# Small per-row numbers of a graph dilation moved from VectorE to GpSimd, one comparison moved between two multiplications, and a joined layer-norm statistic

## The chip, the cores and the metric

The kernel runs on 1 core of one Trainium2 chip. The metric is the device time in microseconds (us) of one execution; of the kernel before there are three timed runs, and one further execution that the hardware profiler recorded. Engines are called by the profile's names: PE (TensorE matmul), PEld (TensorE weight load), DVE (VectorE), ACT (ScalarE), POOL (GpSimd) and SP (SyncE, which issues DMAs).

## The reference

The input is x of shape 16 x 1024 x 128, a dense adjacency of 16 x 1024 x 1024 in f32 with many zeros, and a node mask. Two layers follow each other, each with a layer norm in front and a residual.

```python
h = relu(layernorm(x))
q, k, v = heads(h @ Wq.T + bq), heads(h @ Wk.T + bk), heads(h @ Wv.T + bv)   # 8 heads of 16
attn = softmax(where(adj == 0, -inf, q @ k.T / 4)) * adj
attn = attn / (attn.sum(-1) + 1e-8)
x = x + merge(attn @ v) @ Wo.T + bo

h = relu(layernorm(x))
keep = dilate(adj > 0)            # row after row, see below
for i in 1, 2, 3:                 # SAGE layers on adj * keep
    out = (adj_d @ h / max(adj_d.sum(-1), 1)) @ Wr[i] + h @ Wx[i] + b[i]
    h = batchnorm(relu(out / norm(out))) ; collect h
x = x + concat(h1, h2, h3) @ Wl + bl
```

The dilation goes through the 1024 rows of a batch in turn. Row n has num neighbours; with num > 10 every sf-th of them (sf = (num+1)//2, counted along the row) is removed, with 1 < num <= 10 all are; a removed pair is removed in the row and in the column, so that earlier rows change later ones.

## The kernel before

**Attention.** The outer loop runs over 16 batches b, two halves c of the query columns and eight blocks m of 128 key rows; in each of these 256 turns two groups g of four heads follow each other. That makes 512 steps. In a step PE puts the mask and the scores of four heads into PSUM (L554, L560), ACT takes two exponentials e of 128 x 1024 (L598), DVE multiplies both by the transposed adjacency, giving two weighted exponentials w (L603), and PE multiplies these with the values one step later (L487, and L492 for the small epsilon term). A score tile of the next step is already made while this goes on. Beside it, in pieces, lie the transposes of the adjacency (L505), the next batch's layer norm and projections (`prepare`) and the last half's output projection (`conclude`).

**Dilation.** It runs beside attention as a generator that hands out pieces of DVE work (`dilation`, from L651). All 16 batches are worked on together, in 8 blocks k of 128 rows. A block has three parts:

- Its beginning: products and scans along the diagonal block (L749 to L797), and small numbers per row and batch, 128 x 16 each (`total`, `most`, `half`, `onw`, L774 to L786).
- Seven rounds (L806). A round takes the counts `gone` that PE made (L842), forms num and y from them (L819, L820), from these the position `at16` (L823 to L827), and compares the 128 x 2048 tile w with it (L836, `hit`). PE sums `hit` into the next counts. Some rounds are full ones: they also form `vb` (L830 to L834), by which PE weights two further sums (L846, L847). Full are rounds 2 and 6 in blocks 0 to 4, rounds 0, 2, 4, 6 in block 5, and all in blocks 6 and 7.
- After an end step (L854 to L865) and some wide products, the scan part: for each of the 16 batches a scan over the row (L900), ACT's positions (L915), DVE's removals (L924 to L937) and PE's transposes (L907).

**What sets the order.** PE, ACT and DVE have an order written out by hand; POOL and SP are ordered by the framework. `beside_attention` (L951) runs attention step by step. After each it takes pieces of the dilation as long as their summed cost is behind the share of attention that is done. A piece ends with a `yield` of its cost, of a mark (1: wait for the next attention step; "A" or "B": wait for a step of that parity), and for a comparison also "counts", which makes the next scores stand on PE ahead of the counts. So in the kernel before a round's small numbers and its comparison stand on DVE in front of the step's two w.

**Layer norm.** `layer_norm_relu` takes bn_stats and bn_aggr on DVE for each of eight tiles of 128 x 128, two per step (L274, L276), adds epsilon (L281), takes the power -0.5 on POOL (L282), and ends with the shift on DVE (L284) and the ReLU on ACT (L288).

**The rest.** After attention the three SAGE layers and the output follow (L1107 to L1406); the change does not touch them.

Of the kernel before, what the change touches and what calls it, by code (L numbers as in the profile page):

```python
# [16 lines left out]
ALU = mybir.AluOpType  # L17
# [4 lines left out]
P = 128  # L22
LN_EPS = 1e-5
# [3 lines left out]
ROUNDS = 7  # L27
# [7 lines left out]
def swept(ctx: ExitStack, tc: tile.TileContext, t: dict, out: bass.AP, flag: bass.AP):  # L35
# [8 lines left out]
    nc = tc.nc  # L44
# [122 lines left out]
    def first_part(p1):  # L167
# [100 lines left out]
        def layer_norm_relu(dst, src, name, lo=0, hi=NB):  # L268

            st = shared.tile([P, NB, 6], F32, name=f"st_{name}_{lo}", tag="lnst", bufs=2)  # L270
            mv = shared.tile([P, NB, 2], F32, name=f"mv_{name}_{lo}", tag="lnmv", bufs=2)
            for i in range(lo, hi, 2):
                for j in range(i, i + 2):
                    nc.vector.bn_stats(st[:, j, :], src[:, j, :])  # L274
                for j in range(i, i + 2):
                    nc.vector.bn_aggr(mv[:, j, :], st[:, j, :])  # L276
                if i + 2 < hi:
                    yield False
            rs = shared.tile([P, 2, NB], F32, name=f"rs_{name}_{lo}", tag="lnrs", bufs=2)
            n = slice(lo, hi)  # L280
            nc.vector.tensor_scalar(rs[:, 1, n], mv[:, n, 1], LN_EPS, None, ALU.add)  # L281
            nc.gpsimd.tensor_tensor(rs[:, 0, n], rs[:, 1, n], minus_half[:, n], ALU.pow)  # L282
            yield False
            nc.vector.scalar_tensor_tensor(rs[:, 1, n], mv[:, n, 0], -1.0, rs[:, 0, n], ALU.mult, ALU.mult)  # L284
# [178 lines left out]


        beside = []

        def take_on(steps, at):
            beside.insert(at, [steps, next(steps)])
# [11 lines left out]
        def attention():  # L480
# [86 lines left out]
            for i, (b, c, m) in enumerate(turns):  # L567
# [12 lines left out]
                for g in range(2):  # L580
                    scs = scores(i, g)
                    go_on_with(f"half {c}")
                    if g == 0:
                        go_on_with("first")
                        turning = turn_over(i + 2)
                        next(turning, None)
                    else:
                        go_on_with(True)
                    if late:
                        values(*late)  # L590
                    elif g == 0:
                        go_on_with(True)
                    if (i, g) == (2, 0):
                        node_masks()
                    es, ws = [], []
                    for q in range(2):
                        e = pool.tile([P, 2, HN], F32, name=f"e_{b}_{c}_{m}_{g}_{q}", tag="e", bufs=4)
                        nc.scalar.activation(e, scs[q], AF.Exp, scale=1.0 / math.sqrt(HD))  # L598
                        es.append(e)
                    go_on_with("evict by VectorE")  # L600
                    for q in range(2):
                        w = pool.tile([P, 2, HN], F32, name=f"w_{b}_{c}_{m}_{g}_{q}", tag="w", bufs=4)
                        nc.vector.tensor_tensor(w, es[q], aT.to_broadcast([P, 2, HN]), ALU.mult)  # L603
                        ws.append(w)
                    late = (acc, v1, m, g, es, ws)
                    if m == 0 and g == 0 and i > 0:

                        take_on(conclude(*done), 1 if c == 0 else 0)
                        go_on_with(False)
                    go_on_with("evict")  # L610
                    if g == 0:
                        next(turning, None)
                    go_on_with(False)
                    if i + g + 1 < len(turns):
                        made["next"] = partial(scores, i + g, 1 - g)
                    yield
# [23 lines left out]
        def twice(ap):  # L640

            return ap.unsqueeze(2).to_broadcast([P, B, 2])

        def over_rows(pairs):

            return pairs.unsqueeze(2).to_broadcast([P, B, P // 2, 2])

        def in_pairs(tile_):
            return tile_.rearrange("p b (i t) -> p b i t", t=2)

        def dilation():  # L651
# [84 lines left out]
            for k in range(NB):  # L736
# [32 lines left out]
                for c, hb in enumerate(halves):  # L769
# [1 line left out]
                    for b in range(B // 2):  # L771
                        nc.tensor.transpose(pd[:, b, :], dgs[c][:, b, :], ident_bf)
                    if c == 0:
                        nc.vector.tensor_scalar(onw, w[:, :, P - 1], 1024.0, None, ALU.subtract)  # L774
                        for dg, of in zip(dgs, halves):
                            nc.vector.tensor_reduce(last1[:, of], dg, AX.X, ALU.add)
                    else:

                        nc.vector.tensor_tensor(total, left, right, ALU.add)
                        nc.vector.tensor_tensor(total, total, last1, ALU.add)  # L780
                        nc.vector.tensor_tensor(most, total, kill[:, :, k], ALU.add)
                        nc.vector.tensor_tensor(onw, onw, right, ALU.add)
                        nc.vector.scalar_tensor_tensor(half, total, -0.5, onw, ALU.mult, ALU.add)
                        nc.vector.tensor_scalar(half, half, 0.25, None, ALU.add)
                        end16 = small.tile([P, B, 2], F16, name=f"end16_{k}", tag="at16", bufs=2)
                        nc.vector.tensor_scalar(end16, twice(onw), 1024.0, None, ALU.add)  # L786
# [16 lines left out]
                nc.vector.tensor_copy(mosts, most)  # L803
                nc.vector.tensor_copy(mids, half)
                full = {2, ROUNDS - 1} if k < 5 else {0, 2, 4, ROUNDS - 1} if k == 5 else set(range(ROUNDS))
                for r in range(ROUNDS):  # L806

# [1 line left out]
                    v = small.tile([P, 5, B], F32, name=f"v_{k}_{r}", tag="v", bufs=2)  # L809
                    num, y, c, high, lost = (v[:, i, :] for i in range(5))  # L810
                    if gone is None:
                        nc.vector.tensor_copy(num, most)
                        nc.vector.tensor_copy(y, half)
                    else:
                        if r - 1 in full:
                            rest = gone[:, B : 2 * B]
# [2 lines left out]
                        nc.vector.tensor_tensor(num, mosts, gone[:, :B], ALU.subtract)  # L819
                        nc.vector.scalar_tensor_tensor(y, gone[:, :B], 0.5, mids, ALU.mult, ALU.add)  # L820
                    if r == ROUNDS - 1:
                        nc.vector.tensor_copy(prev, num)
                    nc.vector.tensor_scalar(c, y, MAGIC, MAGIC - 5120.0, ALU.add, ALU.subtract)  # L823
                    nc.vector.tensor_scalar(high, num, 10.5, None, ALU.is_gt)

                    at16 = small.tile([P, B, 2], F16, name=f"at16_{k}_{r}", tag="at16", bufs=2)
                    nc.vector.scalar_tensor_tensor(at16, twice(high), -4096.0, twice(c), ALU.mult, ALU.add)  # L827
                    if r in full:
                        vb = small.tile([P, 2, B, 2], BF, name=f"vb_{k}_{r}", tag="vb", bufs=2)
                        nc.vector.scalar_tensor_tensor(  # L830
                            vb[:, 0], twice(num), 1.5, twice(high), ALU.is_gt, ALU.subtract
                        )
                        nc.vector.scalar_tensor_tensor(c, y, 5120.0, c, ALU.add, ALU.is_gt)
                        nc.vector.tensor_tensor(vb[:, 1], twice(c), twice(high), ALU.mult)  # L834
                    yield (1.6 if r in full else 1.0), (1 if r in (1, 3) else 0)
                    nc.vector.tensor_tensor(in_pairs(hit), in_pairs(w), over_rows(at16), ALU.is_equal)  # L836
                    yield 1.3, 1, "counts"


                    gone = ps_d.tile([P, 512], F32, name=f"gone_{k}_{r}", tag="d")  # L840
# [19 lines left out]
                nc.vector.tensor_scalar(num, num, 0.5, 0.25, ALU.mult, ALU.add)  # L860
                nc.vector.tensor_scalar(num, num, MAGIC, MAGIC, ALU.add, ALU.subtract)
                nc.vector.tensor_scalar(at_odd, num, -3.0, None, ALU.mult)
                nc.vector.tensor_scalar(at_even, num, -3.0, 2.0, ALU.mult, ALU.add)
                nc.vector.scalar_tensor_tensor(off, num, 1.0, high, ALU.add, ALU.mult)
                nc.vector.tensor_scalar(off, off, -1.0, None, ALU.add)  # L865
# [1112 lines left out]
```

## Time and profile before

| What | Value |
|---|---|
| three timed runs, median (lowest, highest) | 3397.52 us (3397.18, 3398.41) |
| the profiled execution's own time | 3396.91 us |
| its span, first to last instruction | 3395.1 us |
| granted TensorE clock | 0.995 |
| two w of a step, each (L603), 1024 of them | 1219 ns, 1205.5 us in all |
| exponential (L598), 1024 of them | 1022 ns, 991.9 us in all |
| comparison of a round (L836), 56 of them | 1219 ns, 68.2 us in all |
| at16 of a round on DVE (L827), 56 of them | 193 ns |
| bn_aggr (L276), 256 of them | 173 ns |
| power on POOL (L282), 33 of them | 65.5 us in all |
| cast of 128 x 16 on POOL (L410), 64 of them | 198 ns |

The page of the profile gives for each engine its busy time as a share of the span, then the span in 40 slices, the DMA queues, the chain that ended last, and the costliest groups of instructions. In this case the chain covers only the last DVE instructions, so that it says nothing of attention. The windows view gives each engine's busy time in a stretch, the timeline gives single instructions in order of time (start, length, engine, line, what it writes and reads, and in brackets the idle time before it with what ended it). Attention's first w starts at 21.1 us, the last at 2321.3 us.

### The profile page before, as it was taken

How to read it: one execution, taken by the hardware profiler on the slowest of the kernel's cores; microseconds unless marked ns; L12 is line 12 of the kernel's file. 1: busy time of each engine (PE TensorE's matmuls, PEld its weight loads, DVE VectorE, ACT ScalarE, POOL GpSimd, SP SyncE). 2: the span in 40 equal slices, each digit the busy share in tenths (PEclk: the TensorE clock that was granted, in tenths of full speed). 3: DMA queues.
4: the chain of work that ended last, by engine and by line, in shares of the span. 5: the costliest groups of instructions: out<-in, count | busy, mean ns of one | idle time of the engine just before them, and what ended most of it. 6: DMA issues, size and time to landing. Idle time of an engine off the chain costs nothing. (4 is left out here: it accounts for less than half of the span.)

```text
span 3395.1 us, 86338 instructions
## 1 busy us (share of the span) xinstructions
PE 3310.6 (98%) x34855; PEld 1872.4 (55%) x34855; DVE 3025.5 (89%) x5399; ACT 2305.4 (68%) x3909; POOL 164.2 (5%) x253
## 2 busy tenths in 40 slices
PE   8999999999999999999999999999999899999997
PEld 3333333333333333333334334336999899999997
DVE  7898989989989998998998999897888899988887
ACT  7699689779879969968976986884232344423334
POOL 2000000000000000000000000000000000000000
PEclk9999999999999999999999999999999999999999
DMA  7357456547637736845863773677999799989996
GB/s 242 108 168 206 137 149 199 161 129 221 188 122 213 221 122 183 238 144 158 236 190 122 237 240 119 189 228 261 346 341 343 284 353 350 353 323 350 352 351 222
DMA packets 650123, 772.28 MB, mean 227 GB/s; under 512 B 173264, under 2 KB 569168, under 8 KB 637424
## 3 DMA queue, kind: packets, MB, share of 16 engines
q1 hardware_dynamic: 632672, 708.58, 64.4%
q0 software_dynamic: 15456, 57.30, 5.0%
q8 instruction: 275, 4.51, 0.6%
q14 instruction: 136, 1.11, 0.1%
q10 hardware_dynamic: 1584, 0.79, 0.1%
HBM read 508.50 MB, written 157.29 MB: 196 GB/s over the span
## 5 line engine op out<-in xcount | busy, mean ns | idle before, releaser
L603 DVE TENSOR_TENSOR w<-e,aT 128x1024 f32<-128x1024 f32 x1024 | 1205.5, 1219 | 138.4 <-ACT e L598 136.8
L598 ACT ACTIVATE e<-sc 128x1024 f32<-128x1024 f32 x1024 | 991.9, 1022 | 333.6 <-PE sc L560 332.6
L1132 PE MATMUL pg<-y,aT 128*128 128x128 f32 (+1 forms) x6144 | 729.8, 275 | 0.0
L1132 PEld LDWEIGHTS pg<-y,aT 128*128 128x128 f32 x6144 | 707.9, 192 | 0.0
L487 PE MATMUL acc<-w,both 128*32 128x512 f32 x4096 | 586.7, 605 | 3.1 <-DVE w L603 2.6
L560 PE MATMUL sc<-qT,kT 32*128 32x512 f32 x4096 | 584.4, 640 | 0.3 <-ACT qT L315 0.3
L492 PE MATMUL acc<-e,eps 128*32 128x512 f32 x4096 | 573.1, 592 | 0.0
L146 DVE SCALAR_TENSOR_TENSOR aT<-mr,aT 128x1024 f32<-128x1024 bf16 x384 | 458.8, 1217 | 0.0
L492 PEld LDWEIGHTS acc<-e,eps 128*32 128x32 f32 x4096 | 150.6, 110 | 294.6 <-issue 289.6
L1155 ACT ACTIVATE sq<-o 128x512 f32<-128x512 f32 x96 | 60.6, 631 | 328.5 <-DVE o L1150 328.5
L554 PEld LDWEIGHTS <-never 32*32 32x32 bf16 x8192 | 80.9, 88 | 347.9 <-issue 325.6
L554 PE MATMUL sc<-nomask,never 32*32 32x512 bf16 x8192 | 252.3, 385 | 16.8 <-ACT e L598 12.3
L1173 ACT COPY hT<-pt 128x512 f32<-128x512 f32 x96 | 56.3, 586 | 289.3 <-PE pt L1169 280.0
L560 PEld LDWEIGHTS sc<-qT,kT 32*128 32x128 f32 x4096 | 160.1, 183 | 116.9 <-issue 116.1
L505 PEld LDWEIGHTS pa<-ident,a 128*128 128x128 f32 x1024 | 107.7, 141 | 181.4 <-issue 129.7
L487 PEld LDWEIGHTS acc<-w,both 128*32 128x32 f32 x4096 | 92.8, 108 | 156.2 <-issue 65.4
L915 ACT ACTIVATE wr<-both,th 128x512 f16<-128x512 f16 x256 | 172.1, 730 | 7.1 <-DVE both L900 6.9
L505 PE MATMUL pa<-ident,a 128*128 128x128 f32 x1024 | 168.3, 287 | 6.4 <-DMA a<-in_adj 5.7
L512 ACT ACTIVATE nomask<-aT 128x512 bf16<-128x512 f32 x256 | 161.4, 630 | 8.1
L1150 DVE SCALAR_TENSOR_TENSOR o<-pg,rdeg,mine 128x128 f32<-128x128 f32 x384 | 108.1, 344 | 55.9 <-PE pg L1132 52.6
L508 ACT COPY aT<-pa 128x512 f32<-128x512 f32 x256 | 152.7, 597 | 5.3 <-PE pa L505 4.3
L900 DVE TENSOR_TENSOR_SCAN both<-rk 128x513 f16<-128x513 bf16 x128 | 155.9, 1218 | 0.0
(228 smaller groups left out, 3894.9 us busy)
## 6 DMA issues: line engine op xcount, KB each, us to landing
aT<-aT_d SPq DMA_DIRECT2D x94, 2048.0 KB, 9.9
mr<-mr_d SPq DMA_DIRECT2D x188, 512.0 KB, 6.0
aT_d<-aT SPq DMA_DIRECT2D x256, 256.0 KB, 4.0
a<-in_adj SPq DMA_DIRECT2D x253, 256.0 KB, 3.7
ad<-in_adj SPq DMA_DIRECT2D x112, 512.0 KB, 4.2
nomask<-nomask SPq DMA_DIRECT2D x512, 96.0 KB, 2.7
nomask<-nomask SPq DMA_DIRECT2D x512, 64.0 KB, 2.7
nomask<-nomask SPq DMA_DIRECT2D x512, 32.0 KB, 2.7
```

What stands on the lines that cost most here:

```text
L146: nc.vector.scalar_tensor_tensor(part, mrs[h][:, j : j + 2, :].rearrange("p j n -> p (j n)"), 0.0, part, ALU.is_equal, ALU.mult)
L487: nc.tensor.matmul(acc[g][32 * j : 32 * j + 32, :], v1[:, m, (2 * j + g) * HW : (2 * j + g) * HW + 32], ws[j // 2][:, j % 2, :], start=(m ...
L492: nc.tensor.matmul(acc[g][32 * j : 32 * j + 32, :], eps8, es[j // 2][:, j % 2, :], start=False, stop=(m == NB - 1),)
L505: nc.tensor.transpose(pa[:, k * P : (k + 1) * P], a[:, k, :], ident)
L512: nc.scalar.activation(nomask[:, 0, :], aT[:, 0, :], AF.Relu, bias=1.0, scale=-1e38, accum_out=zeros[:, i : i + 1])
L554: nc.tensor.matmul(scs[j // 2][to : to + 32, j % 2, :], never[rows, rows], nomask[rows, j, :], start=True, stop=False, tile_position=(32 * ...
L560: nc.tensor.matmul(scs[j // 2][:, j % 2, :], kT[rows, mm], qTs[c][rows, g, :], start=False, stop=True, tile_position=(32 * j, 0),)
L598: nc.scalar.activation(e, scs[q], AF.Exp, scale=1.0 / math.sqrt(HD))
L603: nc.vector.tensor_tensor(w, es[q], aT.to_broadcast([P, 2, HN]), ALU.mult)
L900: nc.vector.tensor_tensor_scan(pair_sums[b % 2], row[:, 0::2], row[:, 1::2], 0.0, ALU.add, ALU.add)
L915: nc.scalar.activation(wrs[b][:, t * HN : (t + 1) * HN], pair_sums[b % 2][:, t : t + HN], AF.Abs, bias=at[:, b : b + 1], scale=2.0,)
L1132: nc.tensor.matmul(pg[:, i // 2, at : at + width], aT[:, j, i * P : (i + 1) * P], y[:, j, :width], start=(j == 0), stop=(j == NB - 1),)
```

## The change

It has four parts.

1. The small 128 x 16 numbers of the dilation are computed by POOL: of a block's beginning, of the rounds (`c`, `high`, `at16`, `vb`) and of the end step. Where DVE had one instruction with two operations on two tensors, POOL has two. What reads PSUM (num, y, the counts) stays on DVE.
2. The comparison of a round is no longer put on DVE at once. It goes into a list `amid`, and attention takes it from there after the first w of its next step, ahead of the second w. Each round now ends with one `yield`, with mark 1, of cost 2.0 (full) or 1.7.
3. The planner's cost of a round is 1.9 instead of 2.5.
4. Layer norm has no bn_aggr: after the last bn_stats of a layer norm, six DVE instructions on 128 x 8 join the statistics of the even and the odd elements for all tiles at once.

```diff
@@ layer_norm_relu
-                for j in range(i, i + 2):
-                    nc.vector.bn_aggr(mv[:, j, :], st[:, j, :])
...
-            nc.vector.tensor_scalar(rs[:, 1, n], mv[:, n, 1], LN_EPS, None, ALU.add)
+            apart, squares = mv[:, n, 0], mv[:, n, 1]
+            nc.vector.tensor_tensor(apart, st[:, n, 1], st[:, n, 4], ALU.subtract)
+            nc.vector.tensor_tensor(squares, st[:, n, 2], st[:, n, 5], ALU.add)
+            nc.vector.scalar_tensor_tensor(apart, apart, D / 4.0, apart, ALU.mult, ALU.mult)
+            nc.vector.tensor_tensor(squares, squares, apart, ALU.add)
+            nc.vector.tensor_scalar(rs[:, 1, n], squares, 1.0 / D, LN_EPS, ALU.mult, ALU.add)
+            nc.vector.tensor_tensor(apart, st[:, n, 1], st[:, n, 4], ALU.add)
             nc.gpsimd.tensor_tensor(rs[:, 0, n], rs[:, 1, n], minus_half[:, n], ALU.pow)
@@ attention, after each w
                         ws.append(w)
+                        while q == 0 and amid:
+                            amid.pop()()
@@ dilation, a block's beginning: seven of its instructions, and L774
-                        nc.vector.tensor_tensor(total, left, right, ALU.add)
+                        nc.gpsimd.tensor_tensor(total, left, right, ALU.add)
...
@@ dilation, a round
-                    nc.vector.tensor_scalar(c, y, MAGIC, MAGIC - 5120.0, ALU.add, ALU.subtract)
-                    nc.vector.tensor_scalar(high, num, 10.5, None, ALU.is_gt)
+                    nc.gpsimd.tensor_scalar(c, y, MAGIC, MAGIC - 5120.0, ALU.add, ALU.subtract)
+                    nc.gpsimd.tensor_scalar(high, num, 10.5, -4096.0, ALU.is_gt, ALU.mult)
                     at16 = small.tile([P, B, 2], F16, name=f"at16_{k}_{r}", tag="at16", bufs=2)
-                    nc.vector.scalar_tensor_tensor(at16, twice(high), -4096.0, twice(c), ALU.mult, ALU.add)
+                    nc.gpsimd.tensor_tensor(at16, twice(high), twice(c), ALU.add)
                     if r in full:
                         vb = small.tile([P, 2, B, 2], BF, name=f"vb_{k}_{r}", tag="vb", bufs=2)
-                        nc.vector.scalar_tensor_tensor(
-                            vb[:, 0], twice(num), 1.5, twice(high), ALU.is_gt, ALU.subtract
-                        )
-                        nc.vector.scalar_tensor_tensor(c, y, 5120.0, c, ALU.add, ALU.is_gt)
-                        nc.vector.tensor_tensor(vb[:, 1], twice(c), twice(high), ALU.mult)
-                    yield (1.6 if r in full else 1.0), (1 if r in (1, 3) else 0)
-                    nc.vector.tensor_tensor(in_pairs(hit), in_pairs(w), over_rows(at16), ALU.is_equal)
-                    yield 1.3, 1, "counts"
+                        nc.gpsimd.tensor_scalar(high, num, 10.5, None, ALU.is_gt)
+                        nc.gpsimd.tensor_scalar(lost, num, 1.5, None, ALU.is_gt)
+                        nc.gpsimd.tensor_tensor(vb[:, 0], twice(lost), twice(high), ALU.subtract)
+                        nc.gpsimd.tensor_tensor(c, y, c, ALU.subtract)
+                        nc.gpsimd.tensor_scalar(c, c, -5120.0, None, ALU.is_gt)
+                        nc.gpsimd.tensor_tensor(vb[:, 1], twice(c), twice(high), ALU.mult)
+                    amid.append(
+                        partial(nc.vector.tensor_tensor, in_pairs(hit), in_pairs(w), over_rows(at16), ALU.is_equal)
+                    )
+                    yield (2.0 if r in full else 1.7), 1, "counts"
+                    while amid:
+                        amid.pop()()
@@ dilation, the end step: L857 to L865, eight instructions become ten
-                nc.vector.tensor_scalar(high, num, 10.5, None, ALU.is_gt)
-                nc.vector.scalar_tensor_tensor(allof, num, 1.5, high, ALU.is_gt, ALU.subtract)
+                nc.gpsimd.tensor_scalar(high, num, 10.5, None, ALU.is_gt)
+                nc.gpsimd.tensor_scalar(allof, num, 1.5, None, ALU.is_gt)
+                nc.gpsimd.tensor_tensor(allof, allof, high, ALU.subtract)
...
@@ beside_attention
-            block = 1.3 + 4.6 + 3.9 + 1.4 + 1.2 + 2.6 + ROUNDS * 2.5 + 2.0 + 5.1 + 1.4 + B * 4.2 + 2.4
+            block = 1.3 + 4.6 + 3.9 + 1.4 + 1.2 + 2.6 + ROUNDS * 1.9 + 2.0 + 5.1 + 1.4 + B * 4.2 + 2.4
```

More of the change, by code (lines that the diff above doesn't have):

```diff
@@ L280, in layer_norm_relu @@
             n = slice(lo, hi)
-            nc.vector.tensor_scalar(rs[:, 1, n], mv[:, n, 1], LN_EPS, None, ALU.add)
+            apart, squares = mv[:, n, 0], mv[:, n, 1]
[5 more added lines that the diff above has]
+            nc.vector.tensor_tensor(apart, st[:, n, 1], st[:, n, 4], ALU.add)
             nc.gpsimd.tensor_tensor(rs[:, 0, n], rs[:, 1, n], minus_half[:, n], ALU.pow)
             yield False
-            nc.vector.scalar_tensor_tensor(rs[:, 1, n], mv[:, n, 0], -1.0, rs[:, 0, n], ALU.mult, ALU.mult)
+            nc.vector.scalar_tensor_tensor(rs[:, 1, n], apart, -0.5, rs[:, 0, n], ALU.mult, ALU.mult)
             for i in range(lo, hi, 2):
@@ L465, in first_part @@
         beside = []
+        amid = []
         def take_on(steps, at):
@@ L773, in dilation @@
                     if c == 0:
-                        nc.vector.tensor_scalar(onw, w[:, :, P - 1], 1024.0, None, ALU.subtract)
+                        nc.gpsimd.tensor_scalar(onw, w[:, :, P - 1], 1024.0, None, ALU.subtract)
                         for dg, of in zip(dgs, halves):
@@ L777, in dilation @@
                     else:
[L779 to L784, printed above, removed]
+                        nc.gpsimd.tensor_tensor(total, left, right, ALU.add)
+                        nc.gpsimd.tensor_tensor(total, total, last1, ALU.add)
+                        nc.gpsimd.tensor_tensor(most, total, kill[:, :, k], ALU.add)
+                        nc.gpsimd.tensor_tensor(onw, onw, right, ALU.add)
+                        nc.gpsimd.tensor_scalar(half, total, -0.5, 0.25, ALU.mult, ALU.add)
+                        nc.gpsimd.tensor_tensor(half, half, onw, ALU.add)
                         end16 = small.tile([P, B, 2], F16, name=f"end16_{k}", tag="at16", bufs=2)
-                        nc.vector.tensor_scalar(end16, twice(onw), 1024.0, None, ALU.add)
+                        nc.gpsimd.tensor_scalar(end16, twice(onw), 1024.0, None, ALU.add)
                     yield (2.5 if c == 0 else 1.4), 1
@@ L802, in dilation @@
                 mosts, mids = parts[:, 0, :], parts[:, 1, :]
-                nc.vector.tensor_copy(mosts, most)
-                nc.vector.tensor_copy(mids, half)
+                nc.gpsimd.tensor_copy(mosts, most)
+                nc.gpsimd.tensor_copy(mids, half)
                 full = {2, ROUNDS - 1} if k < 5 else {0, 2, 4, ROUNDS - 1} if k == 5 else set(range(ROUNDS))
@@ L811, in dilation @@
                     if gone is None:
-                        nc.vector.tensor_copy(num, most)
-                        nc.vector.tensor_copy(y, half)
+                        nc.gpsimd.tensor_copy(num, most)
+                        nc.gpsimd.tensor_copy(y, half)
                     else:
@@ L821, in dilation @@
                     if r == ROUNDS - 1:
-                        nc.vector.tensor_copy(prev, num)
-                    nc.vector.tensor_scalar(c, y, MAGIC, MAGIC - 5120.0, ALU.add, ALU.subtract)
-                    nc.vector.tensor_scalar(high, num, 10.5, None, ALU.is_gt)
+                        nc.gpsimd.tensor_copy(prev, num)
+                    nc.gpsimd.tensor_scalar(c, y, MAGIC, MAGIC - 5120.0, ALU.add, ALU.subtract)
+                    nc.gpsimd.tensor_scalar(high, num, 10.5, -4096.0, ALU.is_gt, ALU.mult)
@@ L856, in dilation @@
                 nc.vector.tensor_tensor(changed[:, k * B : (k + 1) * B], num, prev, ALU.not_equal)
-                nc.vector.tensor_scalar(high, num, 10.5, None, ALU.is_gt)
-                nc.vector.scalar_tensor_tensor(allof, num, 1.5, high, ALU.is_gt, ALU.subtract)
[L860 to L865, printed above, removed]
+                nc.gpsimd.tensor_scalar(high, num, 10.5, None, ALU.is_gt)
+                nc.gpsimd.tensor_scalar(allof, num, 1.5, None, ALU.is_gt)
+                nc.gpsimd.tensor_tensor(allof, allof, high, ALU.subtract)
+                nc.gpsimd.tensor_scalar(num, num, 0.5, 0.25, ALU.mult, ALU.add)
+                nc.gpsimd.tensor_scalar(num, num, MAGIC, MAGIC, ALU.add, ALU.subtract)
+                nc.gpsimd.tensor_scalar(at_odd, num, -3.0, None, ALU.mult)
+                nc.gpsimd.tensor_scalar(at_even, num, -3.0, 2.0, ALU.mult, ALU.add)
+                nc.gpsimd.tensor_scalar(off, num, 1.0, None, ALU.add)
+                nc.gpsimd.tensor_tensor(off, off, high, ALU.mult)
+                nc.gpsimd.tensor_scalar(off, off, -1.0, None, ALU.add)
                 yield 2.0, 1
```

## The prediction, made blind

> **What bounds the kernel now.** I read the page first, then stage windows, then one round of the dilation in the timelines of PE and DVE, then GpSimd (POOL) beside DVE wherever POOL reads SBUF. Page, part 1, and three windows (columns: window, length, busy us of PE, PEld, DVE, ACT, POOL, clock, DMA share, GB/s):
> ```profile
> PE 3310.6 (98%) x34855; PEld 1872.4 (55%) x34855; DVE 3025.5 (89%) x5399; ACT 2305.4 (68%) x3909; POOL 164.2 (5%) x253
> 933.00:971.00 38.00, 37.86 (x532) 14.94 (x525) 35.93 (x82) 26.51 (x43) 3.39 (x4) 1.00 0.38 115
> 2061.00:2103.00 42.00, 42.00 (x713) 19.84 (x706) 38.02 (x96) 25.90 (x42) 1.42 (x4) 1.00 0.38 117
> 1889.00:2027.00 138.00, 132.49 (x1400) 49.42 (x1400) 135.75 (x215) 126.49 (x196) 7.17 (x10) 1.00 0.82 248
> ```
> The first two windows are rounds (blocks 3 and 7), the third is the scan part of block 6. In the rounds PE idles 0.14 and 0.00 us though DVE is at 95% and 91%: DVE work taken out there buys nothing by itself. Only in the scan part does PE idle (5.5 us of 138), with DVE at 98% and ACT at 92%. Attention is 512 steps from 21 to 2322 us, 4.49 us each; what lies behind it (1070 us) the change does not touch.
>
> One round, in block 3 (start us, length, engine, line):
> ```profile
> 957.49 0.55 PE L842 MATMUL gone<-one_bf,hit 128*128 128x1 bf16 x16
> 958.16 0.17 DVE L820 SCALAR_TENSOR_TENSOR v<-gone,parts 128x16 f32<-128x16 f32 x1
> 958.88 1.22 DVE L836 TENSOR_TENSOR hit<-w,at 128x2048 bf16<-128x2048 f16 x1
> 960.02 2.35 DVE L603 TENSOR_TENSOR w<-e,aT 128x1024 f32<-128x1024 f32 x2
> 960.32 0.43 PE L554 MATMUL sc<-nomask,never 32*32 32x512 bf16 x16
> 961.76 0.55 PE L842 MATMUL gone<-one_bf,hit 128*128 128x1 bf16 x16
> ```
> PE's period is 961.76-957.49 = 4.27 us. PE order is count (gone), transposes, weighted values (uses w), next scores, next count. The comparison ends at 960.10, 1.66 us before the count wants it; the two w end at 962.37, 0.37 us before the next values (962.74). That is all the slack.
>
> What POOL does when it reads SBUF beside a two-input DVE instruction:
> ```profile
> 228.47 1.22 DVE L900 TENSOR_TENSOR_SCAN both<-rk 128x513 f16<-128x513 bf16 x1
> 228.71 2.41 POOL L282 TENSOR_TENSOR rs_b<-rs_b,minus_half 128x8 f32<-128x8 f32 x1 [35.86 <-DVE rs_b L281]
> ```
> ```profile
> 896.70 2.28 DVE L756 TENSOR_TENSOR_SCAN w<-go_on,up 128x1024 f16<-128x1024 bf16 x1
> 896.96 3.45 POOL L282 TENSOR_TENSOR rs_a<-rs_a,minus_half 128x8 f32<-128x8 f32 x1 [75.42 <-DVE rs_a L281]
> ```
> ```profile
> 1472.88 1.64 POOL L282 TENSOR_TENSOR rs_a<-rs_a,minus_half 128x8 f32<-128x8 f32 x1 [75.59 <-DVE cs L779]
> ```
> The same pow takes 1.64 us beside 16-element DVE instructions, 2.41 beside a 1.22 us scan, 3.45 beside a 2.28 us scan: in both long cases it ends 1.43 us after the scan does. It is held until the DVE instruction is over, then gets through once, though the next w starts 0.08 us before the scan ends.
>
> **The change part by part.**
> *DVE relieved.* From y (L820) to the comparison DVE loses 958.88-958.33 = 0.55 us in a plain round, 945.70-944.79 = 0.91 in a full one (with vb). 28 of each: 15+25 us. The other small steps of a block: L779 to L786 1.1 us, the end (L857 to L865) 1.3, copies and the rest 0.45, by 8 blocks 23 us. Sum 63 us of DVE, nearly all in stretches where PE never waits: worth 0 at once.
>
> *Order.* The order of the built program has the rounds in consecutive steps, 7 for 7 rounds, where before they took 9. Blocks are 60 steps apart instead of 62, until the pacing spreads the last two scan parts over 56 and 58 steps instead of 54; dilation ends at step 498, not 504. So the densest scans get thinner. PE idle there is 5.5 us (block 6) and 4.8 (block 5, 1594 to 1740), against 3.2 in 131 us of block 1, and matmul groups are stretched by waits by about as much again. I take half of these 20 us, and 2 for the tail: -12 us (0 to -25).
>
> *Layer norm.* Eight bn_aggr at 0.22 us spacing and L281 go (1.1 us), six chained 8-element steps come (four with a 0.2 us dependency, two at 0.09: 1.0 us). Nothing in sum; but it is now one lump after the last pair. Cover: DVE's idle time, 0.4 to 0.6 us a step in the parts without scans. I take 0; without cover 32 lumps cost up to 0.3 each, +10, and 3 us could be gained.
>
> *POOL instructions.* The nearest rows: the 16-element CAST (L410) 198 ns, the 16-element memset (L747) 170 ns. From below bounded by the 1-element memset, 99 ns; from above by the part of pow that does not grow with its elements (1.03 us at 4, 1.64 at 8: 0.43). I take 0.20, plus 0.06 where one waits for another (L746 to L747: 58 ns), 0.15 from DVE to POOL (L281 to L282), 0.03 back.
>
> Here a rule speaks against the change. The Trainium skill, "SBUF — State Buffer", section "Who interferes with whom", says that a DVE instruction with two SBUF inputs and a GpSimd instruction that reads SBUF exclude each other: whichever is second waits for the whole of the first. The pow rows agree (+0.77 and +1.81 us). By the bare 198 ns row the chain of a round, 0.15+4*0.2+0.06 = 1.0 us, hides under the first w (1.22 us) and the change costs nothing. By the rule each POOL step can lose up to one DVE instruction, because w and the comparison both have two SBUF inputs. I replay a round by the rule.
>
> Set y's end to 0. First w: 0.03 to 1.25 if its e is there, else from 0.31 (e is often 0.28 behind y). POOL's first step gets in at the latest at 1.25, the other steps follow while DVE waits for at16: a plain round (3 steps) has at16 at about 1.85, a full one (4) at 2.05 to 2.15. The comparison, queued behind the first w, stalls DVE for 0.5 to 0.85 us; behind it in the queue is the second w, and PE's values wait for that. DVE's period becomes 0.25+1.22+0.6+1.15+1.15 = 4.4 us, more with a bn_stats pair, against PE's 4.3: PE loses 0.25 us per plain round. Where a PSUM-reading step (L407, L429) stands before the first w, it does not block POOL and the stall is covered.
>
> In a full round five more POOL steps follow at16 (high, y-c, vb0, compare, vb1), and PE's count needs both vb. The comparison starts at 2.17, just ahead of them, and holds the first until 3.39; the second w starts at 3.31 and holds the next until 4.53; then three run free: vb1 at 5.4. PE reaches the count at 3.43, ends its first sixteen at 3.84 and then stands, with values, scores and everything else queued behind: 5.4-3.84 = 1.6 us. If one more step slips in at a boundary it is 1.3; at 0.35 us a step it is 2.4; without exclusion 0.
>
> Full rounds with r>0: 2 in each of blocks 0 to 4, 3 in block 5, 6 in 6 and 7, 25 in all. Round 0 has its numbers steps ahead (14 POOL steps of at most 1.4 us in 6.5 PE steps), so does the end of a block (11 steps, about 3.5 PE steps, used after 7). Cost 25*1.6 = 40 us; plain rounds 23*0.25 = 6.
>
> *Other things on POOL's queue.* The pow of a layer norm stands among the rounds about once a block; it starts before the first w, and 1.6 us there falls into the wait for w: 0 to 0.3 us each. rden copies, the go_on memset (queued behind vb, before the end steps) and the few DMA issues have whole steps of slack: 0.
>
> Sum: 40+6-12+0 = +34 us on the profiled execution's 3396.9 (span 3395.1 and 1.8 around it). The median of the runs is 3397.5, 0.6 above: 3431.
>
> **The rivals.**
> *A, forecast: the vb and at16 chains wait for DVE.* 3431, own range 3412 to 3455 (1.3 to 2.0 us a full round, gain 0 to 20). Chance 0.60. For it: every pow that overlaps a scan or comparison is held.
> *B, faster: the chains hide.* If these steps read so early or briefly that they pass between DVE's instructions, the comparison never stalls, DVE's round falls to about 3.9 us, and what stays is the thinner scans and smoother rounds: 3397-12 to -25, say 3381. Chance 0.22. Against it: the pow rows; for it: e comes 0.28 after y in half the rounds, so POOL may take the first turn.
> *C, cancels: only the first step of a chain is held,* the rest run as one stretch. Full rounds lose about 0.4 us, 25*0.4 = 10, less 12: 3396. Chance 0.10.
> *D, much slower: POOL steps of 0.35 to 0.43 us,* each still held. 25*2.5+23*0.7 = 79, less 12: 3464. Chance 0.08.
>
> The slower side decides from about 0.75 us per full round (25*0.75 = 19 against the gain of 12). Within 0.2% (6.8 us, about what a measurement of this kernel can tell from no change) lie C and edges of A and B: faster 0.22, same 0.13, slower 0.65. The range reaches into B and up to D: 3382 to 3464.
>
> **What would show it.** Right: in the profile after, POOL's 16-element steps near 0.2 us alone and over 1 us beside w or the comparison; DVE idle before the comparison, released by POOL; idle PE before the vb matmuls in full rounds, longest in blocks 6 and 7; PE idle of the late scans down. Wrong: vb matmuls following the counts at once, or the comparison starting with no idle time before it, would fell A; a PE loss in the layer-norm steps would show a cost that I put at nothing.

## The result and the profile after

| | before | after |
|---|---|---|
| median of 6 runs each (lowest, highest) | 3398.49 us (3397.18, 3399.55) | 3473.22 us (3467.25, 3478.28) |
| the profiled execution's own time, its span | 3396.91, 3395.1 us | 3474.00, 3472.1 us |
| attention, first w to end of the last w | 2301.4 us | 2374.6 us |
| all behind it | 1072.6 us | 1076.5 us |

The change made the kernel slower: the ratio is 1.0219, with a 95% interval of 1.0206 to 1.0233. That is 75 us where the forecast said 34, and beyond the range (3382 to 3464). Of it 73 us lie in attention, where the change is. What lies behind it takes between 1070.2 and 1077.4 us in all the kept traces, so that its 3.9 us tell nothing.

The page of after, part 1 and the clock's row of part 2:

```profile
PE 3354.1 (97%) x34855; PEld 1883.3 (54%) x34855; DVE 2970.0 (86%) x4888; ACT 2306.4 (66%) x3909; POOL 448.5 (13%) x773
...
PEclk9999999999999999999999999999999999999999
```

DVE lost 55.5 us, POOL gained 284. But PE, with the same 34855 matmuls, is busy for 43.5 us longer. That is the row to stop at: an engine with unchanged work that is busy for longer has been made slower. The 40 slices of the clock hide it, since each is 87 us long. The windows view shows it (window, length, busy us of PE, PEld, DVE, ACT, POOL with numbers of instructions, clock, DMA share, GB/s). Attention before:

```profile
21.10:2322.50 2301.40, 2261.60 (x25737) 839.99 (x25735) 2105.31 (x3516) 1922.92 (x3111) 107.71 (x141) 1.00 0.60 179
```

Attention after, then the rounds of block 7 (42 us again), the scan part of block 6, and one round of block 4 in pieces of 4 us:

```profile
21.10:2395.70 2374.60, 2303.93 (x25740) 849.51 (x25739) 2049.88 (x3006) 1923.95 (x3111) 392.07 (x661) 0.98 0.58 174
...
2093.00:2135.00 42.00, 38.04 (x521) 16.23 (x520) 24.45 (x47) 19.38 (x28) 29.80 (x52) 0.84 0.24 71
...
1889.00:2027.00 138.00, 135.78 (x1412) 49.46 (x1404) 130.56 (x191) 127.91 (x197) 2.64 (x5) 1.00 0.81 243
...
1220.00:1224.00 4.00, 1.53 (x24) 0.64 (x25) 2.21 (x3) 1.94 (x2) 3.52 (x7) 1.00 0.47 143
1224.00:1228.00 4.00, 2.85 (x40) 1.82 (x43) 1.57 (x9) 0.88 (x2) 2.05 (x8) 0.63 0.09 25
1228.00:1232.00 4.00, 4.00 (x36) 1.06 (x32) 3.39 (x3) 0.00 (x0) 0.00 (x0) 0.51 0.00 0
1232.00:1236.00 4.00, 4.00 (x64) 1.52 (x60) 1.93 (x4) 3.14 (x5) 1.86 (x3) 1.00 0.23 66
```

PE idles 2374.60-2303.93 = 70.7 us in attention, before 39.8: 30.9 more. It is busy for 42.3 us longer. Together that is the 73.2 us. The rounds of block 7, where PE had no idle time at all, now have 4.0 us of it in 42 and a mean clock of 0.84. In the round of block 4 PE stands for 2.5 us in the first piece and 1.2 in the second; within the second the clock falls to one half (mean 0.63), and it stays there to the end of the third (0.51), although PE is then busy throughout. The granted clock in the record of attention is at one half for 95.6 us, in 20 stretches of 3.4 or 6.8 us; before there is none.

Why PE stands is seen in the same round on three engines (start us, length, engine, line; idle time before it in brackets). L832 is `high` and L835 `at16`; L838 to L843 are the six steps of `vb`. POOL's order is the framework's: in this round it has put L839 ahead of at16 and L841 ahead of L840. POOL:

```profile
1218.87 1.67 POOL L287 TENSOR_TENSOR rs_a<-rs_a,minus_half 128x8 f32<-128x8 f32 x1 [3.69 <-DVE mv_a L286]
1220.63 0.28 POOL L832 TENSOR_SCALAR v<-v 128x16 f32<-128x16 f32 x1
...
1221.68 0.24 POOL L835 TENSOR_TENSOR at<-v 128x32 f16<-128x32 f32 x1
1222.01 1.30 POOL L838 TENSOR_SCALAR v<-v 128x16 f32<-128x16 f32 x1
1223.38 1.01 POOL L841 TENSOR_TENSOR v<-v 128x16 f32<-128x16 f32 x1
1224.36 0.24 POOL L840 TENSOR_TENSOR vb<-v 128x32 bf16<-128x32 f32 x1
1224.68 0.25 POOL L842 TENSOR_SCALAR v<-v 128x16 f32<-128x16 f32 x1
1225.02 0.24 POOL L843 TENSOR_TENSOR vb<-v 128x32 bf16<-128x32 f32 x1
```

DVE:

```profile
1218.95 1.21 DVE L609 TENSOR_TENSOR w<-e,aT 128x1024 f32<-128x1024 f32 x1
1221.95 1.23 DVE L612 TENSOR_TENSOR hit<-w,at 128x2048 bf16<-128x2048 f16 x1 [1.79 <-POOL at L835]
1223.10 1.22 DVE L609 TENSOR_TENSOR w<-e,aT 128x1024 f32<-128x1024 f32 x1
```

PE:

```profile
1217.60 1.08 PE L493 MATMUL acc<-w,both 128*32 128x512 f32 x8
...
1223.24 0.55 PE L854 MATMUL gone<-one_bf,hit 128*128 128x1 bf16 x16 [2.26 <-DVE hit L612]
1224.65 0.16 PE L858 MATMUL gone<-vb,valid 128*128 128x1 bf16 x1 [0.86 <-POOL vb L840]
1225.31 0.16 PE L859 MATMUL gone<-vb,final 128*128 128x1 bf16 x1 [0.50 <-POOL vb L843]
...
1227.16 1.94 PE L493 MATMUL acc<-w,both 128*32 128x512 f32 x8
```

The first two steps behind at16, L838 and L841, take 1.30 and 1.01 us, the others 0.24 to 0.29. L838 ends 0.13 us after the comparison does, L841 0.07 us after the second w. PE, done with its counts, waits 0.86 us for the first vb and, after one product, 0.50 for the second: 1.36 us. The weighted values L493 after that take 1.94 us, not 1.08. Over all rounds, PE's waits and POOL's groups of after (line, partitions x elements, number | busy us, mean ns | idle before):

```profile
PE gone L858 <- POOL vb L840: 15.1, 18, 0.9
PE gone L854 <- DVE hit L612: 12.7, 16, 2.3
...
PE gone L859 <- POOL vb L843: 11.5, 22, 1.0
```

```profile
L838 POOL TENSOR_SCALAR v<-v 128x16 f32<-128x16 f32 x28 | 30.9, 1104 | 2.5
L841 POOL TENSOR_TENSOR v<-v 128x16 f32<-128x16 f32 x28 | 26.5, 946 | 2.2
...
L840 POOL TENSOR_TENSOR vb<-v 128x32 bf16<-128x32 f32 x28 | 8.7, 312 | 0.0
```

The new waits are 26.6 us for vb and 12.7 for the counts, 39.3 together. PE's idle time elsewhere fell by 39.3-30.9 = 8.4 us, 3.3 of them in the scan window of block 6 alone (5.5 before, 2.2 now).

Which waits are followed by half clock? In 19 of the 56 rounds of this trace PE waited 1.0 us or more in all ahead of vb products (1.26 to 1.36 us in 18 of these, in two waits of at most 1.0 us each), and 18 of the 19 have a stretch at half clock before the next round's counts. Of the other 37 rounds two have one: a round with 1.8 us ahead of its counts, and one with 0.3 us ahead of vb. A round with 1.9 us ahead of its counts has none.

So the wait alone does not decide. Around these waits PE has nothing but products of one column: 16 of them for the counts (L854), 32 with vb (L858, L859). Take the whole stretch, from the last wider matmul ahead of the counts to the first one behind these products. Where it is 3.0 us or longer, half clock follows in 14 of 14 rounds, from 2.0 to 3.0 us in 5 of 7, below that in 1 of 35; before, no such stretch is longer than 1.3 us. In the scan parts PE has 27 waits of 1.0 to 1.6 us in all the kept traces, each ahead of a transpose of 128 columns, and half clock follows none of them. (A wait of 1.2 us ahead of scores, with the order alone, is followed by 3.4 us of it.) The longest of the 27, in the kernel before with the joined layer norm alone:

```profile
1913.32 0.62 PE L912 MATMUL pe<-ident_bf,er 128*128 128x128 bf16 x8 [1.55 <-DVE er L935]
```

That products of one column count for little is the obvious reading; no run changed them, so it is not shown.

### The profile page after: what moved, and what is told of

It reads as the page before. It is cut to its first block, busy times and chain, and to the rows that moved or that the text cites. A ratio compares the mean times of both kernels' runs of the same rounds, so it can differ in the third digit from the quotient of the medians.

```text
span 3472.1 us, 86496 instructions
## 1 busy us (share of the span) xinstructions
PE 3354.1 (97%) x34855; PEld 1883.3 (54%) x34855; DVE 2970.0 (86%) x4888; ACT 2306.4 (66%) x3909; POOL 448.5 (13%) x773
## 5 line engine op out<-in xcount | busy, mean ns | idle before, releaser
L493 PE MATMUL acc<-w,both 128*32 128x512 f32 x4096 | 595.7, 620 | 1.5 <-DVE w L609 1.1
L560 PE MATMUL sc<-nomask,never 32*32 32x512 bf16 x8192 | 255.5, 388 | 15.5 <-ACT e L604 12.0
L493 PEld LDWEIGHTS acc<-w,both 128*32 128x32 f32 x4096 | 91.5, 109 | 155.4 <-issue 81.6
```

Of the source, the lines that this page charges most:

```text
L493: nc.tensor.matmul(acc[g][32 * j : 32 * j + 32, :], v1[:, m, (2 * j + g) * HW : (2 * j + g) * HW + 32], ws[j // 2][:, j % 2, :], start=(m ...
L560: nc.tensor.matmul(scs[j // 2][to : to + 32, j % 2, :], never[rows, rows], nomask[rows, j, :], start=True, stop=False, tile_position=(32 * ...
```

## The experiments

The theory after the result: two instructions of POOL are held one after the other in each full round (as predicted), PE stands some 1.3 us, and nearly each such stand is followed by 3.4 or 6.8 us at half clock, which was in no sum. Rivals: the order or the layer norm costs; POOL's work slows DVE wherever PE waits; the at16 chain is the price. Medians and ratios (95% interval) are against runs of the kernel before on the same chip; PE's idle time and half clock are those of attention in each kernel's profiled execution, all in us; "counts late" and "vb late" are PE's waits ahead of the counts and of the vb products.

| kernel | median us | ratio to before | PE idle | counts late / vb late | half clock |
|---|---|---|---|---|---|
| before | 3395.6 to 3398.5 | 1 | 39.8 | 0 / 0 | 0 |
| order alone | 3396.30 | 0.9999 (0.9990 to 1.0008) | 40.8 | 3.6 / 0 | 3.4 |
| rounds' numbers on DVE | 3396.65 | 1.0001 (0.9992 to 1.0010) | 39.2 | 4.1 / 0 | 3.4 |
| vb on DVE | 3405.49 | 1.0028 (1.0020 to 1.0037) | 41.5 | 8.5 / 0 | 6.8 |
| vb alone on POOL | 3431.69 | 1.0109 (1.0092 to 1.0126) | 52.6 | 2.4 / 16.9 | 37.5 |
| vb products later | 3443.23 | 1.0144 (1.0127 to 1.0160) | 63.2 | 10.5 / 16.0 | 41.0 |
| matmuls in the wait | 3461.59 | 1.0184 (1.0163 to 1.0204) | 60.0 | 15.3 / 9.4 | 30.7 |
| after | 3473.22 | 1.0219 (1.0206 to 1.0233) | 70.7 | 12.7 / 26.6 | 95.6 |

The half clock of one profile is not a fixed number. Three more kernels below have the same POOL chains as after and show 105.8, 75.1 and 88.7 us; the falls to 30.7 to 41.0 us are clear of that. The profile of "vb on DVE" is of its quickest run (3398.73 us, mean clock 0.995); the other twelve have 0.993 or 0.994, so that a usual one holds more half clock than 6.8 us.

**Order alone.** The kernel before with part 2 and part 3 of the change; every small number stays on DVE.

```diff
+                        while q == 0 and amid:
+                            amid.pop()()
...
-                    yield (1.6 if r in full else 1.0), (1 if r in (1, 3) else 0)
-                    nc.vector.tensor_tensor(in_pairs(hit), in_pairs(w), over_rows(at16), ALU.is_equal)
-                    yield 1.3, 1, "counts"
+                    amid.append(
+                        partial(nc.vector.tensor_tensor, in_pairs(hit), in_pairs(w), over_rows(at16), ALU.is_equal)
+                    )
+                    yield (2.0 if r in full else 1.7), 1, "counts"
```

> The kernel before with the new order alone: comparison between the two w, a round per step, planned cost 1.9; all small numbers on VectorE, old layer norm. Theory 1 (the loss is GpSimd's chains, held by VectorE's two-input instructions, and TensorE at half clock after each wait): 3386 us, 3375 to 3400, no half clock in attention. Theory 2 (the order itself loses: rounds in consecutive steps, comparison ahead of the second w): 3430 us or more.

3396.30: no gain. The rounds do close up (from first to last count, summed over eight blocks, 292 us before and 239 here), and the scans of block 6 do get thinner (138-136.72 = 1.3 us of PE idle in a window of 138, 5.5 before). But the comparison now stands behind the first w, and PE waits 3.6 us for it where it never waited. Attention takes 2301.4 us in both.

**Rounds' numbers on DVE.** The changed kernel with the rounds' small numbers put back on DVE. Block edges stay on POOL, and the joined layer norm stays.

> The changed kernel with the rounds' small numbers back on VectorE; a block's beginning and end stay on GpSimd, layer norm stays joined. Theory 1: as the order alone, 3380 to 3395 us, since the beginning and the end have steps of slack on GpSimd. Theory 2: 3440 us or more.

3396.65, 1.7 us above the range expected: block beginnings and end steps on POOL and the joined statistics cost nothing, and the 22 us less DVE work in attention (2082.4 against 2104.7 with the order alone) gain nothing. Everything that the change costs lies in the rounds' numbers.

**vb on DVE.** The changed kernel with c and the four instructions of vb of the full rounds on DVE; the at16 chain stays on POOL (in full rounds without its step c).

```diff
-                    nc.gpsimd.tensor_scalar(c, y, MAGIC, MAGIC - 5120.0, ALU.add, ALU.subtract)
+                    (nc.vector if r in full else nc.gpsimd).tensor_scalar(c, y, MAGIC, MAGIC - 5120.0, ALU.add, ALU.subtract)
...
-                        nc.gpsimd.tensor_scalar(high, num, 10.5, None, ALU.is_gt)
-                        nc.gpsimd.tensor_scalar(lost, num, 1.5, None, ALU.is_gt)
-                        nc.gpsimd.tensor_tensor(vb[:, 0], twice(lost), twice(high), ALU.subtract)
...
+                        nc.vector.scalar_tensor_tensor(
+                            vb[:, 0], twice(num), 1.5, twice(lost), ALU.is_gt, ALU.subtract
+                        )
```

> The changed kernel with vb of the full rounds on VectorE (and c in these rounds), at16 still on GpSimd. Theory 1: the wait of TensorE between counts and vb products goes, the stall of the comparison stays: 3405 to 3435 us, half-clock time under half of the 96 us. Theory 2: 3465 to 3475 us.

3405.49: taking vb away from POOL gives back some 65 of the 75 us. The at16 chain alone costs 9 to 10.

**vb alone on POOL.** The other half: the at16 chain back on DVE, the six vb steps on POOL.

```diff
-                    nc.gpsimd.tensor_scalar(c, y, MAGIC, MAGIC - 5120.0, ALU.add, ALU.subtract)
-                    nc.gpsimd.tensor_scalar(high, num, 10.5, -4096.0, ALU.is_gt, ALU.mult)
+                    nc.vector.tensor_scalar(c, y, MAGIC, MAGIC - 5120.0, ALU.add, ALU.subtract)
+                    nc.vector.tensor_scalar(lost, num, 10.5, None, ALU.is_gt)
...
-                    nc.gpsimd.tensor_tensor(at16, twice(high), twice(c), ALU.add)
+                    nc.vector.scalar_tensor_tensor(at16, twice(lost), -4096.0, twice(c), ALU.mult, ALU.add)
```

> The changed kernel with the chain for the comparison (c, high, at16) back on VectorE; only the six steps of the vb chain stay on GpSimd in the full rounds. Theory (each two-input instruction of VectorE lets one GpSimd step through, so three of them, w, comparison, w, hold the first three steps one after the other): vb lies as far behind the comparison as before, PE waits for vb about 17 us and stays 80 to 100 us at half clock, the comparison no longer waits for GpSimd, time 3455 to 3467. Rival (steps cost their 0.25 to 0.3 us, and the chain starts three steps earlier): the wait for vb shrinks to under 6 us, half clock under 40 us, time 3405 to 3430.

3431.69: between both expectations. POOL's groups of this kernel say why:

```profile
L839 POOL TENSOR_SCALAR v<-v 128x16 f32<-128x16 f32 x28 | 27.6, 987 | 7.5 <-DVE at L835 6.8
L840 POOL TENSOR_TENSOR vb<-v 128x32 bf16<-128x32 f32 x28 | 27.3, 974 | 0.0
L841 POOL TENSOR_TENSOR v<-v 128x16 f32<-128x16 f32 x28 | 25.6, 914 | 0.0
L838 POOL TENSOR_SCALAR v<-v 128x16 f32<-128x16 f32 x28 | 9.3, 333 | 128.0 <-DVE v L828 69.8 <-DVE v L821 55.8 <-DVE v L827 1.5
```

Three steps are held one after the other, by w, comparison and w, as the theory had it. But a fourth, L838, slips in while DVE still computes at16, so that less is left behind the held ones. PE's wait for vb per round falls from 1.26-1.36 to mostly 0.7-0.9 us; in all by a third (26.6 to 16.9), while half clock falls by three fifths (95.6 to 37.5): of 11 rounds with a wait of 0.7 to 0.9 us only 4 are followed by it. The theory had the held steps and the wait right (16.9 us for "about 17"), the half clock and the time wrong; the rival had the half clock right ("under 40") and the rest wrong. So the half clock falls faster than the wait does.

The halves do not add up: at16 alone on POOL costs 9 to 10 us, vb alone 36, both 75. With at16 on POOL the vb steps start later, and fewer of them slip in ahead of the comparison.

**vb products later.** The same POOL work; PE gets a whole step's matmuls between the counts and the vb products, in 14 of the 28 full rounds.

```diff
                     if r in full:
+                        if k < 7 and r < ROUNDS - 1:
+                            yield 0.0, 1
                         for b in range(B):
```

> The changed kernel with the vb products queued on PE one attention step later, behind a step's matmuls, in 14 of the 28 full rounds (the full rounds but the last one of blocks 0 to 6); the same GpSimd work. In the changed kernel's trace these rounds hold about 13 us of the idle time ahead of vb products and about 41 of the 95.6 us at half clock. Theory (the price is PE's idle time and the half clock that follows it, nothing in GpSimd's work itself): the half clock falls to 45 to 65 us, time 3437 to 3452. Rival (GpSimd's steps cost by slowing VectorE, wherever PE waits): 3468 to 3480.

3443.23, half clock 41.0 us (expected 45 to 65), vb waits 16.0. POOL does the same work, and some 27 us are back (47.7 us above the kernel before on its chip, where after was 74.7 above): it is PE's standing, and the half clock behind it, that costs, not POOL's work. None of the 14 changed rounds is followed by half clock here; in after 8 of them are.

**Matmuls in the wait.** The changed kernel with 16 matmuls of 128 columns, whose product nobody reads, between counts and vb products of the full rounds but round 0. They add work; what they take away is PE's standing still.

```diff
                     if r in full:
+                        for _ in range(16 if r else 0):
+                            nc.tensor.matmul(gone[:, 64 : 64 + P], ident_bf, beyond, start=True, stop=True)
                         for b in range(B):
```

> The changed kernel with 16 additional 128-column bf16 matmuls, into unused columns, between the counts and the vb products of each full round but round 0: about 0.9 us of TensorE work that mostly fills a wait. Theory 1: TensorE stays at full clock through those waits; half-clock time falls from 96 us to under 50, and the time to 3440 to 3460 us. Theory 3 (the half clock costs nothing that the waits don't): 3473 to 3490 us, since the matmuls add time where there is no wait.

3461.59, 1.6 us over the range expected, but about 10 below the changed kernel (65.8 us above the kernel before on its chip, not 74.7; the intervals of the ratios just do not touch), although PE works 27.1 us more (the added group's busy time). Half clock falls from 95.6 to 30.7 us. In attention, PE idle +20.2 and the added 27.1 leave 63.8-47.3 = 16.5 us for the half clock.

That residue can be formed for each kernel: attention's length less 2301.4, less PE's additional idle time, less added work, by the us at half clock. It is 42.3/95.6 = 0.44 for after, 15.5/37.5 = 0.41 for vb alone on POOL, 24.5/41.0 = 0.60 for vb products later, 16.5/30.7 = 0.54 here. One half is what half clock would cost a PE that is always busy. What lies above it is something else: with the joined layer norm alone PE is busy for 3.6 us longer in attention without any half clock, so that a few us of each residue are uncertain.

**The layer norm.** Both directions: the changed kernel with bn_aggr put back, and the kernel before with the joined statistics alone.

> The changed kernel with the layer norm's statistics joined by one instruction a chunk again (two aggregating instructions for each pair of chunks), everything else as changed. Theory (the joined statistics neither cost nor gain): 3468 to 3478, as the changed kernel. Rival (the seven longer instructions delay VectorE ahead of a round): 3455 to 3465.

> The kernel of before with the joined statistics of the layer norm alone. Theory: 3393 to 3402, no difference. Rival (VectorE gains what the 64 removed aggregating instructions took): 3380 to 3390.

3469.60, ratio 1.0214 (1.0197 to 1.0231), and 3398.15, ratio 1.0006 (0.9997 to 1.0015). No cost and no gain that can be told.

**The power in front of a round.** In four rounds of after the power of a layer norm stands on POOL directly ahead of the chain (rounds 1, 5, 2, 6 of blocks 1, 2, 4, 5), and in the version with vb on DVE these four hold 7.3 of the 8.5 us that counts are late. First only the power was issued later, in that version and in the changed kernel:

```diff
-            nc.gpsimd.tensor_tensor(rs[:, 0, n], rs[:, 1, n], minus_half[:, n], ALU.pow)
+            powers.append(
+                partial(nc.gpsimd.tensor_tensor, rs[:, 0, n], rs[:, 1, n], minus_half[:, n], ALU.pow)
+            )
```

> The version with the vb chain on VectorE and only the at16 chain on GpSimd (the one that took 3405.5), with each power of a layer norm queued on GpSimd behind the round's numbers of the same step instead of in front of them; nothing else moves. In that version's trace 7.3 of the 8.7 us that PE stands ahead of counts lie in four rounds of 1.8 to 1.9 us each, where a power stood in front of the chain. Theory (what is left of the price is the power, not the at16 chain): the four waits go, 3395 to 3401. Rival (the at16 chain costs by itself, 0.15 us in each of 56 rounds): 3403 to 3408.

> The changed kernel with each power of a layer norm queued on GpSimd behind the round's numbers of the same step. Theory (the power in front of a chain costs about 1.8 us of PE in three or four rounds, and some half clock after it; the rest of the price is the vb chain): 3460 to 3469. Rival (no effect, the vb wait in the same rounds hides it): 3470 to 3478.

3406.62, ratio 1.0024 (1.0015 to 1.0034), and 3470.21, ratio 1.0214 (1.0198 to 1.0230). These two tell nothing: the framework put the power ahead of the chain all the same. POOL in the first of them:

```profile
1194.51 1.67 POOL L990 TENSOR_TENSOR rs_a<-rs_a,minus_half 128x8 f32<-128x8 f32 x1 [3.69 <-DVE mv_a L288]
1196.26 0.50 POOL L838 TENSOR_SCALAR v<-v 128x16 f32<-128x16 f32 x1
```

Then the joining instructions and the power were both moved behind the round's numbers of the step (a function `join` issued after the dilation's pieces):

> Moving the power alone did not change GpSimd's queue: the power still stood in front of the same four rounds' chains. Here, in the version with the vb chain on VectorE (3405.5), the whole lump of a layer norm (the six joining instructions on VectorE and the power) stands behind the round's numbers of the same step on both engines. Theory (these four rounds, blocks 1, 2, 4 and 5, are what is left of the price): PE's time ahead of counts falls from 8.7 to under 4 us, no wait of over 1 us stays, 3396 to 3401. Rival (the at16 chain costs by itself in every round): 3403 to 3408.

> The changed kernel with the whole lump of a layer norm behind the round's numbers of the same step on both engines. Theory (in four rounds the lump and the power cost PE 1.8 to 2.3 us and some half clock; the rest of the price is the vb chain and stays): 3460 to 3469. Rival (the vb wait takes up what is freed there): 3470 to 3478.

3406.15, ratio 1.0026 (1.0016 to 1.0037), and 3472.10, ratio 1.0223 (1.0208 to 1.0239). The counts are late by 4.0 us instead of 8.5 in the first, by 7.5 instead of 12.7 in the second, and the time is the same. The time that the theory expected did not come; the rival's numbers did, but not for its reason, since the counts are not late in every round.

Where do the 9 to 10 us of the at16 chain lie? The version with the power alone issued later keeps the order on POOL and was profiled at its usual time (3406.04 us). Its attention is 9.9 us longer than with the rounds' numbers on DVE: 7.3 us in the rounds (247.6 against 240.3 us from first to last counts, summed over the blocks), 2.6 elsewhere, with 13.7 us at half clock against 3.4. With the lump behind, the rounds take 240.4 us again: within the rounds, these four were the price. But 9.4 us are now lost between the rounds. Its waits (us in total, times, longest) show two places there:

```profile
DVE rk L732 <- DMA gl<-mr_d: 3.9, 2, 3.7
...
PE pd L788 <- DVE valid L804: 2.0, 1, 2.0
```

The first is in the version with the power alone as well:

```profile
1151.08 0.69 DVE L730 SCALAR_TENSOR_TENSOR rk<-rk,gl 128x512 bf16<-128x512 bf16 x1 [3.81 <-DMA gl<-mr_d]
```

That step of attention takes 9.0 us there, and 5.2 in the profile of "vb on DVE", which has no such wait. The kernel before has 2.3 us of it, in three waits. Why the DMA is late in these two, and where the rest between the rounds lies, stays open.

## Why the prediction missed

**What bounds the kernel: right.** DVE work taken out of the rounds bought nothing (rounds' numbers on DVE, against order alone).

**The exclusion of POOL and DVE: right.** The Trainium skill, "SBUF — State Buffer", section "Who interferes with whom", was preferred to the bare 198 ns row, and the trace follows the replay: L838 held by the comparison (1.30 us), L841 let through only at the end of the second w (1.01 us), then three free steps (0.24 to 0.25 us). Rival B is out.

**Step length: a little low.** 0.20 us with 0.06 between; measured free 0.24 to 0.29, with 0.06 to 0.10 between.

**Wait for vb: right in kind, too large.** "25*1.6 = 40 us" is 26.6. The text gave 1.3 us as the case in which "one more step slips in at a boundary", and 1.36 was measured; and in six of the 25 rounds it was 0 to 0.7 us, five of them in blocks 6 and 7, where the text expected the longest.

**Counts late: too small.** "plain rounds 23*0.25 = 6" is 12.7. Only 3.7 of it lie in plain rounds, in just two of them, both with a power in front; 9.0 lie in full rounds, where the sum had no such term.

**The thinner scans: wrong as a gain.** "-12 us (0 to -25)". The scans do get thinner, but the order brings its own wait, for the comparison behind the first w, and the order alone gains 0.

**Layer norm at 0, block edges at 0: right.**

**The power at "0 to 0.3 us each": too small as a wait.** In the round shown it is over at 1220.54, 0.4 us after the first w, and the comparison waits 1.79 us. In the four rounds with a power in front PE waits 6.8 us for its counts: the loss in the layer-norm steps that the text named as a sign of being wrong. Moving the lump took 5 us of PE's waits away, but no time that can be told.

**The step that failed: what PE does after a wait.** The sum took a PE wait for its own length. The waits, 39.3 us of new ones less 8.4 of old, make 30.9 us, near the forecast's 46-12 = 34, in part by luck: the 40 was 26.6, the 6 was 12.7, the 12 was 8.4. The rest of the 73.2 us in attention, 42.3 us, is PE busy for longer: the half clock behind these waits can make up all of it (half of the 95.6 us is 47.8), the two runs that filled or moved the waits took part of it away, and it was nowhere in the sum.

Attention before shows no such stretch. But the trace of before has one 18 us behind attention, where PE stands 1.80 us for DVE and the clock is at half for 3.41 us from 2340.2 on (the last row is the windows view):

```profile
2334.45 1.06 PE L1103 MATMUL pn<-weights,h 128*128 128x128 f32 x8
...
2339.09 0.35 PE L999 MATMUL pf<-still,ones 128*128 128x2 f32 x2 [1.80 <-DVE still L997]
...
2340.59 1.92 PE L1103 MATMUL pn<-weights,h 128*128 128x128 f32 x8
2340.00:2344.00 4.00, 4.00 (x24) 4.00 (x23) 3.66 (x16) 1.71 (x3) 3.19 (x6) 0.57 0.98 414
```

The same eight matmuls take 1.92 us instead of 1.06. So the price could be read off, though not how often it would be paid. The lever was in sight too: the forecast took a PE that stood 0.00 us in the rounds of block 7 to standing 1.6 us every round, and should have carried a term for the clock with two figures. The skill's rule quoted at the end gives 0, since no stand comes near its 3.4 us. The other is an estimate with the window length of the same page ("TensorE: Matmul & The Clock Gate", section "What's actually happening"): half of 3.4 us after each of the 25 full rounds, 43 us. That this comes so near to 42.3 is luck: there were 20 stretches, eight of them twice as long.

Rival D gave 3464 for the wrong reason, steps of 0.35 to 0.43 us.

## What to carry to other kernels

Before moving small steps to GpSimd, ask which two-input VectorE instructions run beside them: each lets about one step through, so a chain's length is counted in those instructions, not in its own steps. If TensorE waits for the end of the chain, price the wait and the half clock behind it, about another 1.4 us per us of new idle time here (42.3 for 30.9). Look for a stand with half clock behind it anywhere in the trace of before, also outside the stage that changes. When an engine with unchanged work is busy for longer, look at its clock in short windows; and give it other work to do in the wait, as queueing the products a step later did for some 27 us.

## What the runs showed of the hardware

A stand well under 3.4 us can be enough for half clock. The Trainium skill, "TensorE: Matmul & The Clock Gate", section "HAM oscillation — how this bites in real kernels", has as its rule that no idle gap should be longer than about 3.4 us. Here no wait in a round was longer than 2.3 us, and half clock came 20 times; in the kernel before it came behind a stand of 1.80 us just after attention. What went with it best in the changed kernel was the whole stretch of waits and products of one column: 3.0 us or more, 14 of 14 rounds; under 2.0 us, 1 of 35. Waits of 1.0 to 1.6 us between wider matmuls, in the scan parts, were followed by none (27 of them). The length of a stretch, 3.4 us or twice that, agrees with the page's window, and its price, half of the throttled time, with the 0.41 to 0.60 found here. How much idle time a window may hold before the clock is halved, no run here settles.
